# Second products for virtual tiles, and byte distances kept in DRAM, in a three-layer graph network kernel

## The chip, the cores and the metric

The kernel runs on one core of one Trainium2 chip. The metric is the device time of one launch, in microseconds, taken as the median of several runs. One further execution was taken with the hardware profiler; its rows are what is read here. The core's engines, with the names that the profile gives them, are TensorE (PE for matmuls, PEld for its weight loads), VectorE (DVE), ScalarE (ACT), GpSimd (POOL) and SyncE (SP), which here only issues DMAs.

## The reference

A graph has 6250 nodes with 128 features each and 200,000 edges, sorted by their destination. After a layer norm and a ReLU, three layers follow. Each takes for every node the maximum, feature by feature, over the rows of its edges' sources (0 where a node has no edge), and puts that and the node's own row through two linear maps. Widths are 128, 256, 256 and 128.

```python
def _sage_conv(x, src, dst, Wl, bl, Wr):
    agg = jax.ops.segment_max(x[src], dst, num_segments=x.shape[0])
    agg = jnp.where(jnp.isfinite(agg), agg, 0.0)
    return agg @ Wl + bl + x @ Wr
...
h = jnp.maximum(_layernorm(x, axis=-1), 0.0)
h = jax.nn.leaky_relu(_sage_conv(h, src, dst, Wl1, bl1, Wr1), NEG_SLOPE)
h = jax.nn.leaky_relu(_sage_conv(h, src, dst, Wl2, bl2, Wr2), NEG_SLOPE)
h = jax.nn.leaky_relu(_sage_conv(h, src, dst, Wl3, bl3, Wr3), NEG_SLOPE)
return x + h
```

Degrees are uneven: destinations are drawn as the square of a uniform number, so the first nodes have far more edges than the last.

## The kernel before

**Tiles.** The nodes lie in 50 tiles of 127 rows (a table row per node, 128 rows per tile). Sources are taken in 25 pairs of tiles, g = 24 down to 0; the two tiles of a pair are its sides s = 0 and 1. Destinations are *units* of 128 columns: 28 narrow ones (tiles 22 to 49), 19 wide ones (tiles 3 to 21), and 8 *virtual* ones. The first three tiles have too many edges for a row, so `virtual` (L621) cuts their edges into rows of 64, 8 x 128 of them, whose maxima are later joined again by a scan along the rows (`Joined`, L1072).

**Two ways to a maximum.** Most edges are taken by *products*. For each unit and pair the kernel keeps one source per destination column (narrow units), or one per side (wide and virtual units, called *alone*). `one_hot` (L897) makes from the stored index bytes a one-hot matrix of up to 1024 columns on ACT, in two passes: Square of (index minus partition) to bf16, then ReLU of 1 minus it. `products` (L908) multiplies it with the pair's rows on PE, split into a high and a low part, so that the product picks rows exactly; `maxima` (L929) takes the running maximum out of PSUM on DVE. An alone step has one maximum for each side, a narrow step one for both.

Edges whose pair (or side) already has a pick are *leaves*. `flag_rows` (L500) marks them, `pick_rows` (L531) collects them by rounds of eight, `rank_rows` (L549) orders the rows by how many they have, and `send_row` (L603) writes them to lists. A list is walked by *gathers* (`Listed.gather`, L961): one indirect DMA on POOL fetches a table row for each of 128 destinations, and a small memset (L974) follows it. `CAPS` (L55) says how many gathers each list row takes: 147, 181, 230 and 47 for lists 0 to 3 by its sums, 605 a layer. `Listed.maximum` (L976) takes maxima over tiles of gathered rows (8 rows deep in layer 0, 4 in layers 1 and 2; L985, and a tree, L990) and stores the result (L994).

**Groups and steps.** Units are worked in four groups: 24 narrow units (group 0), the 8 virtual (group 1), the 19 wide (group 2) and the last 4 narrow (group 3). List k belongs to group k. A step is one chunk of a group for one pair: 8 units in layer 0, 4 in layers 1 and 2. Layer 0 has 75, 25, 75 and 25 steps in its groups, layers 1 and 2 have 150, 50, 125 and 25.

**Order.** The whole order is written out by the program before it runs. An agenda (L1118 to L1269) puts list work, node work and set-up chores on steps; every engine then runs its own instructions in that order. Gathers of lists 0 to 2 are spread evenly over the steps from the start of a layer to shortly before the end of group 2, with an alone step weighted 1.25 in layers 1 and 2; list 3's lie on group 3. `Node` (L997) is the work of one destination tile: an indirect fetch, a transpose, a merge with the products' maxima, the linear maps, the activation, and the stores of its rows for the next layer. Group 0's nodes start when group 0 ends, one every step in layer 0 and one every second step in layers 1 and 2, so they lie on group 1; group 1's joined tiles lie on group 2, and group 2's nodes on group 3. In layer 0 the flags, selections and index lookups of groups 1 to 3 are chores, spread over steps 0 to 82; `expand` and `lookups` (L697, L717) write index bytes to `idx` in DRAM, one row of bytes per pair.

**Queues.** SP issues nearly all plain DMAs in program order: index loads (`load_idx`, L867, a row of bytes broadcast to all partitions, three blocks ahead), pair loads (`load_pair`, L881, two pairs ahead), list results, node loads and stores. One-hots are made up to six steps ahead of their products (`make_hots`, L1294), at most six at a time.

Of the kernel before, what the change touches and what calls it, by code (L numbers as in the profile page):

```python
# [34 lines left out]
BF16 = mybir.dt.bfloat16  # L35
# [7 lines left out]
P = 128  # L43
# [17 lines left out]
DEEP = (24, 40, 48, 24)  # L61
# [7 lines left out]
def kernel(ctx: ExitStack, tc: tile.TileContext, x, src, dst,  # L69
# [28 lines left out]
    )  # L98
    PLACE, HEAD = {}, []
# [42 lines left out]
    IW = [(len(units) + sum(w == "w" for w, _ in units)) * P for units in GROUPS]  # L142
# [226 lines left out]
    rows_w = edge.tile([P, NW + NV, 2 * CUT], I16, name="rows_w")  # L369
    pos_i = edge.tile([P, NV], I32, name="pos_i")  # L370
# [90 lines left out]
    def rows_of(us):  # L461
        w, i = us[0]
        assert [u for u in us] == [(w, i + j) for j in range(len(us))]
        return (rows_n if w == "n" else rows_w)[:, i : i + len(us), :]
# [252 lines left out]
    def lookups(us, least, s, pool, tags=("v", "v8")):  # L717
# [7 lines left out]
        v8 = pool.tile([NG, n * P], U8, tag=tags[1], name="v8", bufs=1 + (tags[0] == "v"))  # L725
        i = 0
        while i < n:
            k = next(k for k, units in enumerate(GROUPS) if us[i] in units)
            m = 1
            while i + m < n and m < 8 and us[i + m] in GROUPS[k]:  # L730
                m += 1
# [5 lines left out]
            at = GROUPS[k].index(us[i]) + (len(GROUPS[k]) if s else 0)  # L737
# [117 lines left out]
    def chunks(layer, k):  # L855

        n = 8 if widths[layer] == P else 4
        units = GROUPS[k]
        for w in "wn":
            us = [i for i, u in enumerate(units) if u[0] == w]  # L860
            for i0 in range(0, len(us), n):
                part = us[i0 : i0 + n]
                yield (HEAD[k] + part[0]) * P, len(part) * P, part[0], units[part[0]][1] if w == "w" else None
# [23 lines left out]
    def parts_of(k):  # L887

        units = GROUPS[k]
        for w in "wn":  # L890
            us = [i for i, u in enumerate(units) if u[0] == w]
            for i0 in range(0, len(us), HOT // P):
                yield us[i0], len(us[i0 : i0 + HOT // P]) * P, len(units) if w == "w" else 0

    hots, live, done_with = {}, [0], [0, 0]

    def one_hot(layer, k, g, c, w, odd, s):  # L897
# [4 lines left out]
        nc.scalar.activation(sq[:, :w], t[:, at : at + w], AF.Square, bias=near[:, s : s + 1], scale=1.0)  # L902
        hot = work.tile([P, HOT], F32R, tag="hot", name="hot", bufs=HOTS)
        nc.scalar.activation(hot[:, :w], sq[:, :w], AF.Relu, bias=1.0, scale=-1.0)  # L904
# [24 lines left out]
    def maxima(step, s, p, acc):  # L929
        layer, k, g, (_, w, c, odd_u) = step  # L930
# [4 lines left out]
        if g == NG - 1 and (odd_u is None or s == 0):  # L935
# [230 lines left out]
    late_lookups(LISTS[1], 1)  # L1166
    n_soon = len(chores)
# [118 lines left out]
    assert max(IW) >= max(g * w for g, w in zip(GB, IW))  # L1286
# [362 lines left out]
```

## Time and profile before

| | us |
|---|---|
| median of 3 runs | 3579.78 |
| lowest and highest | 3576.79, 3585.17 |
| the profiled execution's own time | 3583.85 |
| its span in the profile | 3582.1 |
| stretch up to the first product | 287.8 |
| layer 0 (to the first product of layer 1) | 1083.7 |
| layer 1 | 1110.9 |
| layer 2 and the end | 1099.7 |

A row of a stage gives busy time for each engine; the share that counts is busy time over the length of that stage, since the engines' limits change from group to group. For POOL each gather also costs a short gap before and after it that is not counted as busy. Mean durations mix shapes where a row says "+2 forms".

### The profile page before, as it was taken

What the parts mean: (1) busy time and instruction counts of PE and PEld (TensorE: products, weight loads), DVE (VectorE), ACT (ScalarE), POOL (GpSimd) and SP (SyncE); (2) the same over time, 40 slices, a digit from 0 to 9 for tenths busy, and PEclk for the clock granted to TensorE, in tenths of its full rate; (3) what the DMA queues carried; (4) which work ended last, traced back from release to release, by engine and by line L of the source; (5) the groups of instructions that cost most, each with busy time, mean ns of one, the idle gap of its engine ahead of it and who ended that gap; (6) DMA issues with size and microseconds to landing.
All of it is one profiled execution on the core that took longest, in us unless ns stands there. A gap on an engine that the chain in (4) does not pass through costs nothing.

```text
span 3582.1 us, 37453 instructions
## 1 busy us (share of the span) xinstructions
PE 2378.9 (66%) x8912; PEld 1680.0 (47%) x8912; DVE 2594.4 (72%) x4077; ACT 2460.1 (69%) x3433; POOL 2837.5 (79%) x4030
## 2 busy tenths in 40 slices
PE   1025632557567567888778687769888777677767
PEld 1013421334334335666555455547666555455545
DVE  6557899987556535666667899955666678799964
ACT  5108952769779758998655587757998856477754
POOL 5578894888888873888876788883888888878884
PEclk9986865769767779999889899989999989899989
DMA  9114320338644366555577665578555567565566
GB/s 288 43 20 111 100 76 14 93 98 265 155 129 125 109 188 184 157 171 159 183 227 233 174 186 175 167 212 281 163 162 165 157 212 239 159 168 171 172 188 195
DMA packets 295272, 579.84 MB, mean 162 GB/s; under 512 B 58529, under 2 KB 155669, under 8 KB 294403
## 3 DMA queue, kind: packets, MB, share of 16 engines
q1 hardware_dynamic: 203331, 347.72, 29.7%
q0 software_dynamic: 91648, 229.44, 24.6%
q8 instruction: 75, 1.23, 0.1%
q14 instruction: 154, 1.26, 0.1%
q10 hardware_dynamic: 64, 0.20, 0.0%
HBM read 486.57 MB, written 90.55 MB: 161 GB/s over the span
## 4 chain that ended last, share of the span: by engine, by line
POOL 27%; DVE 22%; PE 14%; issue 14%; ACT 10%; DMA 10%; another core or an unknown queue 1%; SPq 1%; POOLq 0%; DVEq 0%; ACTq 0%
POOL g L970 18%; DVE acc L938 8%; PE pg L921 8%; POOL pace_t L974 7%; ACT sq L902 6%; DMA g<-table,let 5%; ACT hot L904 3%; PE z_p L1043 2%; DVE g L985 2%; DVE g L990 1%; PE z_p L1045 1%; DVE acc L541 1%; DVE acc L539 1%; DMA agg<-best,end_i 1%
## 5 line engine op out<-in xcount | busy, mean ns | idle before, releaser
L921 PE MATMUL pg<-hot,pair_sb 128*128 128x512 f32 x7000 | 2045.9, 440 | 540.3 <-DVE acc L938 243.4
L970 POOL DMA_INDIRECT g<-table,let x1815 | 1830.8, 1009 | 451.0 <-issue 285.2
L921 PEld LDWEIGHTS pg<-hot,pair_sb 128*128 128x128 f32 x7000 | 1397.5, 212 | 1050.5 <-ACT hot L904 293.7
L938 DVE TENSOR_TENSOR acc<-acc,pg 128x1024 f32<-128x1024 f32 (+3 forms) x1314 | 1488.5, 1161 | 309.0 <-PE pg L921 205.9
L904 ACT ACTIVATE hot<-sq 128x1024 fp32r<-128x1024 bf16 (+2 forms) x1200 | 1126.5, 939 | 367.8 <-PE pg L921 298.4
L902 ACT ACTIVATE sq<-idx_sb,near 128x1024 bf16<-128x1024 uint8 (+2 forms) x1200 | 1218.7, 1016 | 15.5 <-POOL pace_t L974 15.5
L974 POOL MEMSET pace_t<- 128x300 bf16 x1815 | 664.0, 366 | 0.9
L985 DVE TENSOR_TENSOR g<-g 128x1024 f32<-128x1024 f32 (+4 forms) x277 | 290.6, 1049 | 209.9 <-DMA g<-table,let 192.8
L1047 ACT COPY s<-z_p 127x256 f32<-127x256 f32 (+1 forms) x150 | 49.9, 333 | 368.4 <-PE z_p L1045 230.6
L990 DVE TENSOR_TENSOR g<-g 128x256 f32<-128x256 f32 (+3 forms) x355 | 175.7, 495 | 83.1 <-DMA g<-table,let 55.9
L1014 POOL DMA_INDIRECT agg<-best,end_i x141 | 140.5, 997 | 95.2 <-PE aT_p L1030 35.5
L959 ACT ACTIVATE let<-ell 128x4 int32<-128x4 int16 (+3 forms) x516 | 92.8, 189 | 86.9 <-DMA ell<-picks 86.9
L1030 PE MATMUL aT_p<-ident,agg 128*128 128x128 f32 x250 | 57.7, 297 | 141.4 <-DMA agg<-best,end_i 112.2
L1043 PE MATMUL z_p<-wr,hT_in 128*128 128x256 f32 (+1 forms) x500 | 148.6, 418 | 4.6 <-DMA hT_in<-across 4.5
L1036 DVE TENSOR_TENSOR mz<-acc,aT_p 128x256 f32<-128x256 f32 (+1 forms) x141 | 52.4, 371 | 131.3 <-PE aT_p L1030 89.3
L1045 PE MATMUL z_p<-wl,mz 128*128 128x256 f32 (+1 forms) x500 | 121.1, 359 | 8.0 <-DVE mz L1036 3.6
L1030 PEld LDWEIGHTS aT_p<-ident,agg 128*128 128x128 f32 x250 | 34.3, 148 | 170.2 <-DMA agg<-best,end_i 114.6
L605 POOL DMA_INDIRECT picks<-picked,to_i x55 | 59.3, 1078 | 64.7 <-DVE rank_h L581 48.1
L1043 PEld LDWEIGHTS z_p<-wr,hT_in 128*128 128x128 f32 x500 | 86.9, 217 | 34.2 <-issue 12.7
L1045 PEld LDWEIGHTS z_p<-wl,mz 128*128 128x128 f32 x500 | 92.3, 210 | 20.9 <-DVE mz L1036 4.4
L830 PE MATMUL hT_p<-ident,h 128*128 128x128 f32 x200 | 44.9, 309 | 82.8 <-DVE mz L1036 44.3
L348 POOL DMA_INDIRECT win_d<-in_dst_dram,win_i x50 | 52.3, 1046 | 44.0 <-ACT junk_w L353 14.7
(259 smaller groups left out, 1133.5 us busy)
## 6 DMA issues: line engine op xcount, KB each, us to landing
pair_sb<-pair SPq DMA_DIRECT2D x200, 512.0 KB
idx_sb<-idx SPq DMA_DIRECT2D x75, 608.0 KB
g<-table,let POOLq DMA_INDIRECT x1815
idx_sb<-idx SPq DMA_DIRECT2D x75, 384.0 KB
pair_sb<-pair SPq DMA_DIRECT2D x100, 256.0 KB
pair<-pr SPq DMA_DIRECT2D x100, 256.0 KB
idx_sb<-idx SPq DMA_DIRECT2D x75, 256.0 KB
best<-g SPq DMA_DIRECT2D x110, 128.0 KB
```

The costliest lines, as they stand in the source:

```text
L902: nc.scalar.activation(sq[:, :w], t[:, at : at + w], AF.Square, bias=near[:, s : s + 1], scale=1.0)
L904: nc.scalar.activation(hot[:, :w], sq[:, :w], AF.Relu, bias=1.0, scale=-1.0)
L921: nc.tensor.matmul(to, pr[:, s, i, kk * P : (kk + 1) * P], hot[:, o : o + bw], start=((alone or s == 0) and i == 0), stop=((alone or s == ...
L938: nc.vector.tensor_max(to, to, of)
L959: nc.scalar.activation(let[:, :n], ell[self.k][:, q, j : j + n], AF.Identity, scale=1.0)
L970: nc.gpsimd.indirect_dma_start(out=self.tiles[q, b][:, i, :], out_offset=None, in_=tables[self.layer], in_offset=bass.IndirectOffsetOnAxis ...
L974: nc.gpsimd.memset(pace_t, 0.0)
L985: nc.vector.tensor_max(base[:, : i + 1, :], base[:, : i + 1, :], g[:, : i + 1, :])
L990: nc.vector.tensor_max(base[:, :h, :], base[:, :h, :], base[:, w - h : w, :])
L1014: nc.gpsimd.indirect_dma_start(out=self.agg[:, : self.F], out_offset=None, in_=of, in_offset=bass.IndirectOffsetOnAxis(ap=at, axis=0),)
L1043: nc.tensor.matmul(z_p, self.hT[:, i, :], wr[layer][:, i, :], start=False, stop=False)
L1045: nc.tensor.matmul(z_p, self.m[:, i, :], wl[layer][:, i, :], start=False, stop=(i == K - 1))
```

## The change

Virtual units get a *second product*. Where two or more edges of a virtual row have their source in the same pair and side beyond the first picks, one more of them per pair is taken out of the leaves and put into a row of its own, `rows_x`. `EXTRA` holds 8 further units ("x", v), which share the accumulator columns of the virtual units; `PLANES` is `GROUPS` with these added to group 1. An x unit is worked like a narrow one (one pick for both sides, one maximum a step). So list 1 gets shorter: its `CAPS` row sums to 86 in place of 181, and its depth `DEEP` is 24 in place of 40. Group 1 has 50 steps in layer 0 and 100 in layers 1 and 2. Its one-hots go from two to four for each pair, and the x units' lookup is one more chore, before step 40.

The second part changes how one-hots are made. In layer 0 the first pass is Abs to bytes (`away`, three buffers) in place of Square to bf16; the second pass reads these bytes. Each tile of bytes is also stored to DRAM (`far`) by SP, at the time when the next one-hot is issued. In layers 1 and 2 `load_idx` loads these distances, for both sides, in place of the broadcast index bytes, and a one-hot is the second pass alone.

```diff
-    (37, 30, 29, 27, 26, 23, 8, 1),
+    (22, 15, 14, 12, 11, 9, 2, 1),
...
-DEEP = (24, 40, 48, 24)
+DEEP = (24, 24, 48, 24)
...
+    EXTRA = [("x", v) for v in range(NV)]
+    PLANES = [units + (EXTRA if k == 1 else []) for k, units in enumerate(GROUPS)]
...
+    DW = [2 * len(units) * P for units in PLANES]
+    far = [dram.tile([P, NG, DW[k]], U8, name=f"far{k}") for k in range(len(GROUPS))]
...
+        if wide and us[0][1] >= NW:
+            c, seen = S(1, I32, n, J), S(2, I32, n, J)
+            nc.vector.memset(b[:, :, J - 1 :], 0)
+            nc.vector.tensor_copy(c, b)
+            repeated(seen, c, J)
+            nc.vector.tensor_tensor(b, b, c, op=OP.bitwise_xor)
+            x = rows_of([("x", i - NW) for _, i in us])
+            nc.vector.tensor_scalar(f, b, 0.0, float(PAST), op0=OP.is_equal, op1=OP.mult)
+            nc.vector.tensor_tensor(x, f, r[:, :, :J], op=OP.max)
+            nc.vector.tensor_scalar(f, b, 0.0, float(PAST), op0=OP.not_equal, op1=OP.mult)
+            nc.vector.tensor_tensor(r[:, :, :J], f, r[:, :, :J], op=OP.max)
+            b = c
...
-        n, w = len(gs), IW[k]
+        n, w = len(gs), DW[k] if layer else IW[k]
...
+        if layer:
+            nc.sync.dma_start(t[:, : n * w].rearrange("p (g w) -> p g w", w=w), far[k][:, g0 : g0 + n, :])
+        elif n == 1:
...
-        at = of + (c + (odd if s else 0)) * P
-        sq = work.tile([P, HOT], BF16, tag="sq", name="sq", bufs=2)
-        nc.scalar.activation(sq[:, :w], t[:, at : at + w], AF.Square, bias=near[:, s : s + 1], scale=1.0)
+        put = 2 * c * P + s * w
+        if layer == 0:
+            at = of + (c + (odd if s else 0) + (NV if PLANES[k][c] in EXTRA else 0)) * P
+            away = work.tile([P, HOT], U8, tag="away", name="away", bufs=3)[:, :w]
+            nc.scalar.activation(away, t[:, at : at + w], AF.Abs, bias=near[:, s : s + 1], scale=1.0)
+            if unsent:
+                nc.sync.dma_start(*unsent.pop())
+            unsent.append((far[k][:, g, put : put + w], away))
+        else:
+            away = t[:, of + put : of + put + w]
         hot = work.tile([P, HOT], F32R, tag="hot", name="hot", bufs=HOTS)
-        nc.scalar.activation(hot[:, :w], sq[:, :w], AF.Relu, bias=1.0, scale=-1.0)
+        nc.scalar.activation(hot[:, :w], away, AF.Relu, bias=1.0, scale=-1.0)
...
     late_lookups(LISTS[1], 1)
+    late_lookups(EXTRA, 0)
     n_soon = len(chores)
```

More of the change, by code (lines that the diff above doesn't have):

```diff
@@ L141 @@
     cols = dram.tile([P, T], I16, name="cols")
-    IW = [(len(units) + sum(w == "w" for w, _ in units)) * P for units in GROUPS]
+    IW = [(len(units) + sum(w == "w" for w, _ in units)) * P for units in PLANES]
     GB = (1, 1, 1, 5)
     idx = [dram.tile([NG, IW[k]], U8, name=f"idx{k}") for k in range(len(GROUPS))]
+    DW = [2 * len(units) * P for units in PLANES]
+    far = [dram.tile([P, NG, DW[k]], U8, name=f"far{k}") for k in range(len(GROUPS))]
     picks = [dram.tile([len(LISTS[k]) * P, DEEP[k]], I16, name=f"picks{k}") for k in range(NL)]
@@ L369 @@
     rows_w = edge.tile([P, NW + NV, 2 * CUT], I16, name="rows_w")
+    rows_x = edge.tile([P, NV, CUT], I16, name="rows_x")
     pos_i = edge.tile([P, NV], I32, name="pos_i")
@@ L463, in rows_of @@
         assert [u for u in us] == [(w, i + j) for j in range(len(us))]
-        return (rows_n if w == "n" else rows_w)[:, i : i + len(us), :]
+        return {"n": rows_n, "w": rows_w, "x": rows_x}[w][:, i : i + len(us), :]
     def count_of(us):
@@ L724, in lookups @@
             nc.vector.tensor_scalar(v, v, float(P), None, op0=OP.add)
-        v8 = pool.tile([NG, n * P], U8, tag=tags[1], name="v8", bufs=1 + (tags[0] == "v"))
+        v8 = pool.tile([NG, n * P], U8, tag=tags[1], name="v8")
         i = 0
         while i < n:
-            k = next(k for k, units in enumerate(GROUPS) if us[i] in units)
+            k = next(k for k, units in enumerate(PLANES) if us[i] in units)
             m = 1
-            while i + m < n and m < 8 and us[i + m] in GROUPS[k]:
+            while i + m < n and m < 8 and us[i + m] in PLANES[k]:
                 m += 1
@@ L736, in lookups @@
             nc.scalar.copy(part.rearrange("g (c k) -> g c k", k=P), p[:, :m, :])
-            at = GROUPS[k].index(us[i]) + (len(GROUPS[k]) if s else 0)
+            at = NV + PLANES[k].index(us[i]) if us[i] in EXTRA else GROUPS[k].index(us[i]) + (len(GROUPS[k]) if s else 0)
             nc.sync.dma_start(idx[k][:, at * P : (at + m) * P], part)
@@ L857, in chunks @@
         n = 8 if widths[layer] == P else 4
-        units = GROUPS[k]
-        for w in "wn":
+        units = PLANES[k]
+        for w in "wnx":
             us = [i for i, u in enumerate(units) if u[0] == w]
@@ L862, in chunks @@
                 part = us[i0 : i0 + n]
-                yield (HEAD[k] + part[0]) * P, len(part) * P, part[0], units[part[0]][1] if w == "w" else None
+                yield part[0] - (NV if w == "x" else 0), len(part) * P, part[0], units[part[0]][1] if w == "w" else None
     pair_q, idx_q = {}, {}
     def load_idx(layer, k, gs):
-        n, w = len(gs), IW[k]
-        assert stored[k] == w
-        t = work.tile([P, max(IW)], U8, tag="idx", name="idx_sb", bufs=AHEAD + 1)
+        n, w = len(gs), DW[k] if layer else IW[k]
+        assert stored[k] == IW[k]
+        t = work.tile([P, max(DW)], U8, tag="idx", name="idx_sb", bufs=AHEAD + 1)
         g0 = min(gs)
-        if n == 1:
+        if layer:
+            nc.sync.dma_start(t[:, : n * w].rearrange("p (g w) -> p g w", w=w), far[k][:, g0 : g0 + n, :])
+        elif n == 1:
             nc.sync.dma_start(t[:, :w], idx[k][g0 : g0 + 1, :].partition_broadcast(P))
@@ L887, in parts_of @@
     def parts_of(k):
-        units = GROUPS[k]
-        for w in "wn":
+        units = PLANES[k]
+        for w in "wnx":
             us = [i for i, u in enumerate(units) if u[0] == w]
             for i0 in range(0, len(us), HOT // P):
-                yield us[i0], len(us[i0 : i0 + HOT // P]) * P, len(units) if w == "w" else 0
+                yield us[i0], len(us[i0 : i0 + HOT // P]) * P, len(GROUPS[k]) if w == "w" else 0
     hots, live, done_with = {}, [0], [0, 0]
+    unsent = []
     def one_hot(layer, k, g, c, w, odd, s):
         t, of = idx_q[layer, k, g]
-        at = of + (c + (odd if s else 0)) * P
-        sq = work.tile([P, HOT], BF16, tag="sq", name="sq", bufs=2)
-        nc.scalar.activation(sq[:, :w], t[:, at : at + w], AF.Square, bias=near[:, s : s + 1], scale=1.0)
+        put = 2 * c * P + s * w
[8 more added lines that the diff above has]
+            away = t[:, of + put : of + put + w]
         hot = work.tile([P, HOT], F32R, tag="hot", name="hot", bufs=HOTS)
-        nc.scalar.activation(hot[:, :w], sq[:, :w], AF.Relu, bias=1.0, scale=-1.0)
+        nc.scalar.activation(hot[:, :w], away, AF.Relu, bias=1.0, scale=-1.0)
         hots[layer, k, g, c, s] = hot
@@ L929, in maxima @@
     def maxima(step, s, p, acc):
-        layer, k, g, (_, w, c, odd_u) = step
+        layer, k, g, (c, w, _, odd_u) = step
         if widths[layer] // P == 2:
@@ L934, in maxima @@
             of, to = p.rearrange("p h c -> p (h c)")[:, :w], acc[:, 0, c * P : c * P + w]
-        if g == NG - 1 and (odd_u is None or s == 0):
+        if g == NG - 1 and c == step[3][2] and (odd_u is None or s == 0):
             nc.vector.tensor_copy(to, of)
@@ L1285 @@
                 jobs_h.append((at_step[layer, k, g, c], len(blocks) - 1, (layer, k, g, c, w, odd, s)))
-    assert max(IW) >= max(g * w for g, w in zip(GB, IW))
+    assert max(DW) >= max(g * w for g, w in zip(GB, DW)) and max(DW) >= max(g * w for g, w in zip(GB, IW))
     loaded = [0]
@@ L1298, in make_hots @@
             _, b, job = jobs_h.pop(0)
+            if job[0] and unsent:
+                nc.sync.dma_start(*unsent.pop())
             load_until(b + 1 + AHEAD)
```

2 lines of the change are left out of this document (1 added, 1 removed).

## The prediction

> **What bounds the kernel now.** I read the page's busy times first, then the granted clock and busy time of each stage, then groups, then single instructions. A *stage* is one group of one layer. Its bounds come from counting L921's 7000 matmuls off in program order: 600, 200, 500, 100 in layer 0 and 1200, 400, 1000, 200 in layers 1 and 2. On the page no engine stands out:
>
> ```profile
> PE 2378.9 (66%) x8912; PEld 1680.0 (47%) x8912; DVE 2594.4 (72%) x4077; ACT 2460.1 (69%) x3433; POOL 2837.5 (79%) x4030
> ```
>
> By stage it is otherwise. The rows below give: stretch, length, busy us of PE, PEld, DVE, ACT, POOL (instructions), granted clock, DMA share, GB/s. In order: layer 0 group 0 up to step 40, its rest, groups 1, 2, 3; then groups 0, 1, 2, 3 of layer 1 and of layer 2.
>
> ```profile
> 287.80:464.90 177.10, 119.25 (x343) 72.15 (x343) 142.62 (x333) 173.36 (x203) 156.90 (x233) 0.80 0.34 99
> 464.90:756.00 291.10, 109.22 (x324) 71.98 (x325) 273.50 (x720) 155.34 (x176) 215.05 (x313) 0.65 0.22 59
> ...
> 756.00:904.50 148.50, 102.52 (x378) 65.78 (x377) 112.01 (x231) 125.83 (x184) 123.83 (x173) 0.86 0.73 216
> 904.50:1246.10 341.60, 206.05 (x568) 132.12 (x566) 193.49 (x251) 279.83 (x401) 300.44 (x441) 0.72 0.44 124
> 1246.10:1371.50 125.40, 75.08 (x252) 44.10 (x253) 45.77 (x106) 75.88 (x152) 81.65 (x112) 0.74 0.67 198
> 1371.50:1735.20 363.70, 310.53 (x1235) 240.69 (x1233) 240.09 (x249) 331.56 (x390) 298.16 (x435) 0.94 0.54 160
> 1735.20:1972.10 236.90, 182.40 (x701) 130.55 (x702) 168.85 (x199) 127.57 (x192) 177.75 (x251) 0.86 0.75 227
> 1972.10:2357.40 385.30, 291.94 (x1084) 199.22 (x1083) 358.65 (x362) 274.62 (x396) 330.43 (x477) 0.93 0.59 174
> 2357.40:2482.40 125.00, 102.35 (x444) 76.95 (x445) 63.78 (x97) 75.41 (x152) 79.92 (x107) 0.90 0.89 277
> 2482.40:2851.90 369.50, 312.02 (x1258) 241.70 (x1256) 241.75 (x251) 335.23 (x395) 297.94 (x435) 0.95 0.54 160
> 2851.90:3049.20 197.30, 143.53 (x656) 104.27 (x657) 163.81 (x199) 110.49 (x146) 172.35 (x238) 0.91 0.71 228
> 3049.20:3444.20 395.00, 295.91 (x1076) 202.27 (x1074) 358.37 (x361) 269.48 (x384) 341.36 (x490) 0.90 0.56 165
> ```
>
> The gathers' pace comes from the timeline of layer 2's group 0, with an ACT one-hot pair beside it:
>
> ```profile
> 2604.03 0.95 POOL L970 DMA_INDIRECT g<-table,let  x1 [0.16 <-issue]
> ...
> 2605.51 0.95 POOL L970 DMA_INDIRECT g<-table,let  x1 [0.16 <-issue]
> ...
> 2604.12 1.13 ACT L902 ACTIVATE sq<-idx_sb,near 128x1024 bf16<-128x1024 uint8 x1
> 2605.28 1.06 ACT L904 ACTIVATE hot<-sq 128x1024 fp32r<-128x1024 bf16 x1
> 2606.25 1.13 ACT L902 ACTIVATE sq<-idx_sb,near 128x1024 bf16<-128x1024 uint8 x1
> ...
> 2609.95 0.95 POOL L970 DMA_INDIRECT g<-table,let  x1 [0.17 <-issue]
> ...
> 2612.26 1.23 DVE L985 TENSOR_TENSOR g<-g 128x1024 f32<-128x1024 f32 x1 [3.51 <-DMA g<-table,let]
> ```
>
> A gather takes 1.48 us (2604.03 to 2605.51); a one-hot of 1024 columns takes 2.13 us of ACT in two passes (2604.12 to 2606.25). The plan puts 558 gathers on the steps of groups 0 to 2. Gathers per stage:
>
> ```profile
> 756.00:904.50 148.50, 69.81 (x71) 0.86 0.73 216
> 904.50:1246.10 341.60, 210.89 (x214) 0.72 0.44 124
> ...
> 1371.50:1735.20 363.70, 219.52 (x218) 0.94 0.54 160
> 1735.20:1972.10 236.90, 112.58 (x114) 0.86 0.75 227
> 1972.10:2357.40 385.30, 235.22 (x233) 0.93 0.59 174
> ```
>
> So group 0 of layers 1 and 2 is paced by POOL (218 x 1.48 = 323 of 364 us) with ACT close behind (332). Group 2 is paced by DVE (359 of 385) and POOL (233 x 1.48 = 345 and 11 joined fetches). Group 1 is full on no engine. In layer 0, group 0 is ACT-bound up to step 40 (173 of 177) and DVE-bound after it (273 of 291, the chores); group 2 is POOL's (214 x 1.48 = 317 of 342) with ACT at 280.
>
> **The change, part by part.** *Gathers.* List 1 falls from 181 to 86, lists 0 to 2 from 558 to 463 a layer. Group 1 gets twice the steps, so the same plan spreads fewer gathers over more steps: weighted steps go from about 354 to 404 in layers 1 and 2 (143 in group 0, 62.5 to 112.5 in group 1, 149 in group 2), 1.58 to 1.15 gathers a step. In layer 0 it is 3.1 to 2.2.
>
> *Group 0, layers 1 and 2.* POOL: 143 x 1.15 x 1.48 = 243 us. ACT: one pass, 150 x 1.06 and the lets, under 190. DVE loses some 13 list maxima, about 225. PE is next: 1200 matmuls, whose dense pitch and busy time are
>
> ```profile
> 2603.60 9.33 PE L921 MATMUL pg<-hot,pair_sb 128*128 128x512 f32 x40 [0.59 <-ACT sq L902]
> ...
> 1371.50:1735.20 363.70, 305.44 (x1201) 0.94 0.54 160
> ```
>
> 0.233 us each in the burst (9.33 / 40), 0.254 by busy time (305 / 1201, which counts pipeline tails of short bursts). 1200 x 0.233 = 280, with 16 for the four nodes of the layer before (an estimate from the rows of a node below) 296, over 0.975 for waits 304. That is -61 in layer 1 and -64 in layer 2, each between -76 (no waits) and -44 (0.254). I take the burst, since the waits for gathers and one-hots that break bursts now are what goes. [...]
>
> *Group 2, layers 1 and 2.* Its maxima stay; gathers go to 149 x 1.15 = 171, POOL to 265, so DVE alone paces it. About 17 list maxima of 1.22 us leave: -20 each (0 to -35).
>
> *Group 1, layers 1 and 2.* Added: per layer 400 matmuls, 50 one-hots of one pass and 50 maxima of 128x1024; 25 pair steps are now 50. The nodes of group 0 hang here, one to two steps, and turn in a ring:
>
> ```profile
> 1907.93 2.35 DVE L938 TENSOR_TENSOR acc<-acc,pg 128x1024 f32<-128x1024 f32 x2 [2.85 <-PE z_p L1045]
> 1910.20 1.22 DVE L985 TENSOR_TENSOR g<-g 128x1024 f32<-128x1024 f32 x1
> 1911.34 0.42 DVE L1054 SCALAR_TENSOR_TENSOR h<-s 127x256 f32<-127x256 f32 x1
> ...
> 1912.14 0.44 PE L830 MATMUL hT_p<-ident,h 128*128 128x128 f32 x2 [2.19 <-DVE mz L1036]
> ...
> 1914.00 2.08 PE L1043 MATMUL z_p<-wr,hT_in 128*128 128x256 f32 x4
> 1915.87 1.36 PE L1045 MATMUL z_p<-wl,mz 128*128 128x256 f32 x4
> ...
> 1918.20 2.35 DVE L938 TENSOR_TENSOR acc<-acc,pg 128x1024 f32<-128x1024 f32 x2 [2.86 <-PE z_p L1045]
> ```
>
> DVE waits for PE, PE for DVE, 10.3 us a turn here, 9.5 on average (236.9 / 25). A turn of two second-product steps has one maximum fewer in the ring: 8.3. 24 nodes take 12 turns of each: 214. The other 52 steps, 13 pairs of tiles, have no node: six maxima at 1.16 (4.65 us for four on this timeline, 2.35 for two above) and five gathers' share of list maxima, 8.5 us of DVE, 8.9 with waits, 116 in all. 330 for 237: +93. In layer 2 a turn is 7.9 (197.3 / 25) and 6.7: 175 + 116 = 291 for 197, +94. Bounds: below, PE's busy time and 93 more (275, 236: +38, +39); above, the free steps at group 2's and group 0's present pace (385 / 125 and 364 / 150), +121. I take the ring, nearest to what the rows show.
>
> *Group 1, layer 0.* One-hots stay at two passes (Abs to bytes for Square) and double: 50 more of 2.13 us, 107 of ACT onto 126 busy of 148. Some 26 steps with nodes stay at 5.9 (154), 24 steps without at 4.6 (two one-hots, lets): 264, +116 (+85 by ACT alone, +149 at the present pace throughout). *Group 2, layer 0:* POOL falls to about 220, so ACT's 280 paces it, 304 with its joined nodes, -38 (-20 to -60). *Group 0, layer 0:* ACT up to step 40 is as it was. The x lookup adds some 21 us of DVE:
>
> ```profile
> L703 DVE TENSOR_SCALAR acc<-rows_w 128x384 int16<-128x384 int16 (+2 forms) x200 | 63.3, 380 | 0.2
> L709 DVE TENSOR_TENSOR acc<-acc 128x960 int16<-128x960 int16 (+4 forms) x130 | 61.8, 475 | 4.5
> ...
> L710 DVE TENSOR_REDUCE least<-acc 128x30 int16<-128x240 int16 (+3 forms) x45 | 19.5, 433 | 1.6
> ```
>
> (145 us for 54 wide units' sides and a few narrow ones, 2.6 each, eight more). It lies before step 40, where DVE is idle 34 of 177 us. The extra flags and the two selection rounds saved per row of list 1 I set against each other. After step 40 fewer list maxima: -5 (-20 to +20). Group 3 everywhere hangs on nodes: 0, and -2 where ACT has one pass.
>
> *Stores and the added wait.* Layer 0 stores 450 tiles of bytes (52 MB) from SP. SP waits for each Abs, and behind it stand index, pair and node loads and best stores; an Abs waits for the store three before. At 2.13 us a one-hot that leaves 3 x 2.13 - 1.13 = 5.3 us. Nearest row: the gather issued at 2609.95, as large (128 rows of 1 KB), had landed by 2612.26, 2.3 us. Hidden, then. Loads of distances: 768 KB for 384 in group 0, but nine gathers of 128 KB a pair become seven: 2.2 MB in 12 us is 180 GB/s, below the 277 seen in group 3.
>
> **Sum.** Layer 0: -5 + 116 - 38 = +73; layer 1: -61 + 93 - 20 - 2 = +10; layer 2: -64 + 94 - 20 - 2 = +8. +91 on the profiled execution's 3583.85 us (span 3582.1) is 3675. That execution is 4 us above the median shown, so 3671.
>
> **Rivals.** *Faster: the added steps fill the ring's waits.* PE waits 2.2 us and DVE 2.9 in each turn; if matmuls and maxima of the new steps slip in there, group 1 costs only its fullest engine: +38, +39 and +85 in place of +93, +94 and +116, in all -50: 3530. It decides once a new step adds less than 1.9 us of PE. Against it: engines run in program order, and nodes are bound to steps, not to time; the free steps come after. 0.14. *PE is not next in group 0.* Then POOL's 243 paces it, 254 with waits, 50 less in each layer: 3571. Against it: no burst is denser than 0.23 us. 0.04. [...] *Stores hold ACT in layer 0.* With SP held elsewhere, as it is now,
>
> ```profile
> SPq L994 <- DVE g L990: 912.1, 122, 35.5
> ```
>
> landings of 6.5 us make a one-hot 2.54 us, 0.4 more on some 330: +132, 3803. From 5.3 us it decides; 2.3 speaks against. 0.10. *One pass buys little:* the doubled bytes or DVE's waits for gathers keep group 0 half way: +62, 3733. 0.08.
>
> **How the numbers follow.** Forecast 0.62 (3620 to 3725, the bounds of group 1 and group 0 not all on one side), the rest unnamed. Range 3565 to 3745: it takes in the second rival and the fourth, leaves out most of the first and the third. A measurement of this kernel tells 0.2% (7 us) from nothing. Faster: 0.14, half of the second, a little of the forecast's lower end: 0.18. Same: 0.06. Slower: 0.76.
>
> **What would show it.** Layer 1 group 0 near 304 us with PE above 0.9 busy; group 1 near 330 with free steps at 2.2 us and DVE full; layer 0 group 1 near 264 with ACT full; layer 0 group 2 ACT-bound. POOL, with 285 gathers fewer, should be near 0.67 busy over the span. Wrong if group 1 of layer 1 is under 290, or POOL still paces group 0, or Abs waits for DMA.

## The result and the profile after

The changed kernel took 3522.2 us (median of four runs, 3516.2 to 3531.8) against 3579.6 for the kernel before (four runs, 3576.8 to 3585.2): a ratio of 0.984, interval 0.9814 to 0.9867. It is faster by 1.6%, where 2.5% slower was forecast. The profiled execution took 3516.2 us (span 3514.4), 68 less than that of before. Of these 68, 22 lie in the stretch up to the first product (287.8 before, 265.8 after), and are not the change's doing: four kernels run on one chip, with second products and without, all have 266 to 270 there.

First the page's busy times (engine, busy us, share of the span, instructions), then the windows of the changed kernel cut at the same places as in the prediction: groups 0 to 3 of layer 0, of layer 1 and of layer 2, the columns as there.

```profile
PE 2570.8 (73%) x9920; PEld 1816.2 (52%) x9920; DVE 2686.4 (76%) x4152; ACT 1894.1 (54%) x2762; POOL 2444.0 (70%) x3460
```

```profile
265.80:771.10 505.30, 250.72 (x674) 149.34 (x675) 415.72 (x1053) 330.22 (x361) 297.06 (x436) 0.68 0.37 102
771.10:1032.80 261.70, 181.13 (x603) 111.31 (x601) 151.20 (x274) 234.44 (x304) 175.69 (x252) 0.86 0.73 205
1032.90:1323.10 290.20, 194.45 (x540) 118.40 (x540) 181.97 (x232) 270.44 (x363) 224.62 (x330) 0.78 0.60 176
1323.10:1439.20 116.10, 79.44 (x253) 44.66 (x253) 45.63 (x105) 81.23 (x163) 61.49 (x81) 0.77 0.83 243
1439.20:1724.10 284.90, 282.69 (x1234) 231.63 (x1233) 224.88 (x231) 162.65 (x220) 226.93 (x331) 0.99 0.69 213
1724.10:2019.30 295.20, 264.66 (x1113) 194.39 (x1112) 236.38 (x264) 127.42 (x208) 208.66 (x292) 0.98 0.76 219
2019.30:2383.50 364.20, 290.52 (x1073) 196.05 (x1071) 340.65 (x339) 139.66 (x222) 261.07 (x376) 0.93 0.52 163
2383.50:2489.80 106.30, 99.17 (x445) 74.86 (x446) 63.48 (x97) 44.78 (x105) 61.86 (x81) 0.97 0.98 328
2489.80:2774.50 284.70, 283.79 (x1258) 232.79 (x1257) 226.67 (x233) 163.70 (x223) 228.52 (x336) 1.00 0.70 218
2774.50:3020.90 246.40, 231.45 (x1065) 173.17 (x1064) 229.35 (x264) 108.42 (x160) 205.77 (x287) 1.00 0.76 222
3020.90:3382.70 361.80, 284.22 (x1066) 190.90 (x1065) 340.01 (x339) 137.47 (x216) 259.38 (x378) 0.94 0.52 161
3382.70:3514.40 131.70, 93.34 (x457) 70.70 (x457) 66.33 (x116) 30.72 (x73) 62.22 (x79) 0.86 0.68 202
```

Read the length against the fullest engine, row by row. Group 0 of layers 1 and 2 is now PE's alone: 282.7 busy of 284.9. Group 2 is DVE's (341 of 364). Group 1 has no full engine, but PE stands at 265 of 295 in layer 1, at a clock of 0.98 where it was 0.86 before, and at 231 of 246 in layer 2. The two tables side by side:

| stage | before | after | measured | forecast |
|---|---|---|---|---|
| start and layer 0, group 0 | 756.0 | 771.1 | +15 | -5 |
| layer 0, group 1 | 148.5 | 261.7 | +113 | +116 |
| layer 0, group 2 | 341.6 | 290.2 | -51 | -38 |
| layer 0, group 3 | 125.4 | 116.1 | -9 | 0 |
| layer 1, group 0 | 363.7 | 284.9 | -79 | -61 |
| layer 1, group 1 | 236.9 | 295.2 | +58 | +93 |
| layer 1, group 2 | 385.3 | 364.2 | -21 | -20 |
| layer 1, group 3 | 125.0 | 106.3 | -19 | -2 |
| layer 2, group 0 | 369.5 | 284.7 | -85 | -64 |
| layer 2, group 1 | 197.3 | 246.4 | +49 | +94 |
| layer 2, group 2 | 395.0 | 361.8 | -33 | -20 |
| layer 2, group 3 | 137.9 | 131.7 | -6 | -2 |
| sum | | | -68 | +91 |

In the first row group 0 itself rose by 37 (468.2 to 505.3); the shorter start hides 22 of it. The forecast is 159 us too high. Half of that, 80, is group 1 of layers 1 and 2; 39 is their group 0, 21 their group 3, 14 their group 2, and 5 is layer 0 with the start before it.

Group 1 splits into the part with nodes and the free steps behind it. These are the two windows of layer 1:

```profile
1724.10:1912.20 188.10, 165.33 (x710) 121.77 (x709) 134.87 (x171) 73.22 (x138) 119.91 (x165) 0.96 0.74 219
1912.20:2019.30 107.10, 99.33 (x405) 72.62 (x404) 101.50 (x93) 54.20 (x70) 88.74 (x128) 1.00 0.79 219
```

The 50 free steps take 2.14 us each (forecast 2.2) with DVE nearly full, 101.5 of 107.1. The nodes' part (the other 50 steps) takes 188 where 214 was forecast for 48. So the free steps were sized rightly, and the ring was not.

Before, a turn of the ring lasted 10.26 us in the rows of the prediction (from the matmul of `wr` at 1914.00 to the next at 1924.26). These windows of the kernel before cut the same stretch every 3.41 us (length, PE's busy time, clock, DMA share, GB/s):

```profile
1902.88:1906.29 3.41, 3.41 (x9) 0.50 0.90 276
1906.29:1909.70 3.41, 3.41 (x17) 1.00 0.87 262
1909.70:1913.11 3.41, 1.22 (x7) 1.00 0.23 82
1913.12:1916.53 3.41, 3.41 (x9) 0.50 0.83 278
1916.53:1919.94 3.41, 3.41 (x17) 1.00 0.86 255
1919.94:1923.35 3.41, 1.23 (x7) 1.00 0.36 121
```

The clock goes 0.50, 1.00, 1.00 and again: one window in three at half, in step with the turn (three windows are 10.24 us). The slow window stands behind the one in which PE, after waiting 2.19 us for DVE, was busy for only 1.22 us of 3.41. In these turns the node's matmuls fall into the slow one: four of them took 2.08 us there, at 0.50. PE's longest wait in a turn was 2.19 us. With the profile cut on the same grid (its records of the clock begin at 230 us, after the change at 211), the clock is 0.50 or 1.00 in 982 windows of 983 (in all 968 after the change). What tells slow windows from fast ones in these traces is how long PE was busy in the window before: a full-speed window in which PE was busy for less than 40% was followed by a half-speed one in 86 cases of 86, one with more than 60% in none of 488; between the two both occur (51 half, 63 full). After the change it is 44 of 44 and none of 581.

In the changed kernel the timeline of PE has this, in a stretch of the same kind:

```profile
1843.93 1.13 PE L1070 MATMUL z_p<-wr,hT_in 128*128 128x256 f32 x4
...
1849.97 0.44 PE L847 MATMUL hT_p<-ident,h 128*128 128x128 f32 x2 [1.05 <-DVE mz L1063]
...
1851.47 1.13 PE L1070 MATMUL z_p<-wr,hT_in 128*128 128x256 f32 x4
...
1856.37 0.44 PE L847 MATMUL hT_p<-ident,h 128*128 128x128 f32 x2
...
1857.88 1.13 PE L1070 MATMUL z_p<-wr,hT_in 128*128 128x256 f32 x4
```

The same four matmuls take 1.13 us, at a clock of 1.00. A turn of two alone steps is 7.54 us (1843.93 to 1851.47), one of two second-product steps 6.41 (to 1857.88). PE's wait for DVE is 1.05 us in the first and gone in the second; it was 2.19. A single wait of 1.05 us leaves PE busy for some 69% of a window (an estimate from 1.05 of 3.41). What left DVE's side is the list maximum ahead of `h` (1910.20 in the prediction's rows, 1.14 us until `h` starts at 1911.34). In this turn after the change there is none:

```profile
1846.89 2.35 DVE L965 TENSOR_TENSOR acc<-acc,pg 128x1024 f32<-128x1024 f32 x2 [1.51 <-PE pg L948]
1849.16 0.42 DVE L1081 SCALAR_TENSOR_TENSOR h<-s 127x256 f32<-127x256 f32 x1
1849.50 0.41 DVE L1063 TENSOR_TENSOR mz<-acc,aT_p 128x256 f32<-128x256 f32 x1
```

So of the 2.72 us between the turns (10.26 to 7.54), 1.14 are the list maximum and the other 1.58 go with the clock.

### The profile page after: what moved, and what is told of

It is laid out like the page before. It is cut to its first block, busy times and chain, and to the rows that moved or that the text cites. A ratio compares the mean times of both kernels' runs of the same rounds, so it can differ in the third digit from the quotient of the medians.

```text
span 3514.4 us, 39180 instructions
## 1 busy us (share of the span) xinstructions
PE 2570.8 (73%) x9920; PEld 1816.2 (52%) x9920; DVE 2686.4 (76%) x4152; ACT 1894.1 (54%) x2762; POOL 2444.0 (70%) x3460
## 5 line engine op out<-in xcount | busy, mean ns | idle before, releaser
L948 PE MATMUL pg<-hot,pair_sb 128*128 128x512 f32 (+1 forms) x8000 | 2257.3, 429 | 536.5 <-ACT hot L931 249.6
L948 PEld LDWEIGHTS pg<-hot,pair_sb 128*128 128x128 f32 x8000 | 1540.3, 204 | 1124.2 <-ACT hot L931 442.3
L997 POOL DMA_INDIRECT g<-table,let x1530 | 1543.9, 1009 | 765.6 <-ACT let L986 320.7
L965 DVE TENSOR_TENSOR acc<-acc,pg 128x1024 f32<-128x1024 f32 (+3 forms) x1439 | 1647.2, 1168 | 484.1 <-PE pg L948 338.3
L931 ACT ACTIVATE hot<-idx_sb 128x1024 fp32r<-128x1024 uint8 (+2 forms) x900 | 827.0, 948 | 732.8 <-PE pg L948 463.1
L924 ACT ACTIVATE away<-idx_sb,near 128x1024 uint8<-128x1024 uint8 (+2 forms) x450 | 464.4, 1032 | 210.1 <-DMA far<-away 178.0
L1001 POOL MEMSET pace_t<- 128x300 bf16 x1530 | 560.3, 366 | 1.0
L931 ACT ACTIVATE hot<-away 128x1024 fp32r<-128x1024 uint8 (+2 forms) x450 | 427.7, 951 | 14.3
L1012 DVE TENSOR_TENSOR g<-g 128x1024 f32<-128x1024 f32 (+6 forms) x218 | 219.6, 1007 | 1.6 <-DMA g<-table,let 1.5
L1017 DVE TENSOR_TENSOR g<-g 128x512 f32<-128x512 f32 (+3 forms) x351 | 172.9, 493 | 10.2
```

Source lines behind the costliest of these rows:

```text
L924: nc.scalar.activation(away, t[:, at : at + w], AF.Abs, bias=near[:, s : s + 1], scale=1.0)
L931: nc.scalar.activation(hot[:, :w], away, AF.Relu, bias=1.0, scale=-1.0)
L948: nc.tensor.matmul(to, pr[:, s, i, kk * P : (kk + 1) * P], hot[:, o : o + bw], start=((alone or s == 0) and i == 0), stop=((alone or s == ...
L965: nc.vector.tensor_max(to, to, of)
L997: nc.gpsimd.indirect_dma_start(out=self.tiles[q, b][:, i, :], out_offset=None, in_=tables[self.layer], in_offset=bass.IndirectOffsetOnAxis ...
L1001: nc.gpsimd.memset(pace_t, 0.0)
```

## The experiments

Each run is compared with the kernel before on the same chip; whole times of different chips are not set against each other, since the kernel before had medians from 3532.9 to 3596.0 us in the four sets of runs. Stage lengths are, with two cautions. The same layer 0 took 1083.7 us in the kernel before and 1102.7 in a kernel below (the one with matmuls that nobody reads) that differs from it in layer 1 alone, so some 20 us between chips say nothing there. And group 1 of layer 1 took 288.8 to 302.8 us in six kernels whose layers 1 and 2 are the same. "Layer 0" below is without the start, which differs by chip (235 to 237 us in one set, 264 to 270 in two others): 1083.7 for before, 1173.4 after.

**The two parts apart.** The second products alone, with two-pass one-hots everywhere:

```diff
...
+        sq = work.tile([P, HOT], BF16, tag="sq", name="sq", bufs=2)
+        nc.scalar.activation(sq[:, :w], t[:, at : at + w], AF.Square, bias=near[:, s : s + 1], scale=1.0)
...
-        nc.scalar.activation(hot[:, :w], away, AF.Relu, bias=1.0, scale=-1.0)
+        nc.scalar.activation(hot[:, :w], sq[:, :w], AF.Relu, bias=1.0, scale=-1.0)
```

> The second products alone: one-hots in two passes in all layers, index bytes loaded as before, no distances stored. Theory A (each part lifts one of two limits that lie close together: POOL and ACT in group 0 of layers 1 and 2): group 0 of layer 1 stays near 345 us, since ACT's two passes (150 x 2.13 us and the lets) now pace it alone; group 1 of layer 1 near 300; 3590 to 3630 us in all, slower than before. Rival B (the gathers were the limit and the second pass was hidden): group 0 near 290 us, total 3490 to 3530.

And the distances alone:

```diff
-    (22, 15, 14, 12, 11, 9, 2, 1),
+    (37, 30, 29, 27, 26, 23, 8, 1),
...
-DEEP = (24, 24, 48, 24)
+DEEP = (24, 40, 48, 24)
...
-    EXTRA = [("x", v) for v in range(NV)]
+    EXTRA = []
...
```

> The stored distances alone: no second products, lists of 558 gathers in groups 0 to 2 as before, one pass in layers 1 and 2. Theory A: POOL alone paces group 0 of layers 1 and 2 (218 gathers of 1.48 us, 323 us): 330 to 345 us each against 364 and 369; group 2 hardly moves; layer 0 up to 15 us longer by its stores; 3530 to 3560 us in all. Rival B' (ACT was the limit): group 0 near 290 us, total 3440 to 3480.

Second products alone: 3572.5 us, ratio 0.9927 (0.99 to 0.9954), a little faster where slower was expected. Distances alone: 3636.0, ratio 1.0104 (1.0081 to 1.0126), slower where faster was expected. The ratios multiply to 1.003; together the parts give 0.984. Group 0 of layer 1 shows why. This is its window with second products alone, and group 1's behind it:

```profile
1376.10:1706.80 330.70, 302.81 (x1235) 225.34 (x1234) 226.78 (x231) 322.59 (x364) 225.30 (x330) 0.99 0.52 156
1706.80:2005.20 298.40, 267.03 (x1113) 196.19 (x1112) 236.35 (x264) 239.51 (x313) 199.31 (x287) 0.97 0.72 206
```

And with distances alone, group 0:

```profile
1422.60:1786.60 364.00, 305.90 (x1235) 237.61 (x1233) 239.49 (x249) 164.92 (x237) 299.46 (x435) 0.95 0.60 184
```

ACT halved (165) and 364.0 us, as before: POOL still paces the stage. It stands until 1449.1, 26 us into the stage, in a wait of 36.9 us for ACT (a list's indices), and from there runs 337 us with some 2 us of waits for other engines; the 330 to 345 expected left that standing time out. POOL relieved (225): 330.7, and now ACT paces it, at 323. Both: 284.9, and PE paces it. Two limits close to each other have to go together, and the gain of each alone says little. Group 1 of layer 1 is 298.4 without any change to its one-hots, so its 295 does not come from the one pass. In layer 0 the second products alone give 1105.8 (group 0 472.9, then 251.0, 278.4, 103.5), the distances alone 1155.3, and there the distances only cost.

**The list's length by itself.** The changed kernel with list 1 as long as before, 95 gathers a layer more; the added ones fetch the floor row, and two small constant tiles lie in another pool for room:

```diff
-    (22, 15, 14, 12, 11, 9, 2, 1),
+    (37, 30, 29, 27, 26, 23, 8, 1),
...
-DEEP = (24, 24, 48, 24)
+DEEP = (24, 40, 48, 24)
...
```

> The whole change, but with the list lengths of before (181 gathers for list 1, the ones too many fetch the floor row): second products without fewer gathers. Theory C (the nodes' turn in group 1 got short because PE's clock stays up): group 1 of layer 1 stays at 290 to 305 us and its clock above 0.95; group 0 near 300 us by POOL (about 195 gathers); total 3570 to 3600 us. Rival D (the turn got short because fewer list maxima stand in it): group 1 of layer 1 at 320 us or more.

One run: 3767.4 us, span 3765.6, far above the 3570 to 3600 expected; group 0 of layer 1 takes 329.0 where 300 was expected. Stage by stage it is 251 us above the changed kernel (65 in layer 0, 89 and 97 in layers 1 and 2): 0.88 us for each of 285 gathers. So it is the shorter list that pays for the second products. Whether gathers of many rows would cost as much as these, which all fetch one, was not measured. Group 1 of layer 1:

```profile
1833.80:2153.60 319.80, 276.37 (x1114) 202.43 (x1113) 244.20 (x269) 127.68 (x215) 237.31 (x338) 0.93 0.84 210
```

319.8 against 295.2 (288.8 to 302.8 in the six), at 0.93 against 0.98: with the gathers the list maxima are back, and with them half-clock time. (Half-clock time, an estimate, is 2 x (1 - clock) x length, with the clock taken as 0.50 or 1.00 as in the windows above: 66 us in this group before, 12 after, 45 here.) A theory that the clock alone was cured by denser matmuls expected over 0.95 here; it fails.

**Clock or list maximum?** Into the kernel before, eight matmuls whose product nobody reads, ahead of each transpose of group 0's nodes in layer 1:

```diff
+            if self.layer == 1 and self.k == 0:
+                f_p = psum.tile([P, 512], F32, tag="z", name="f_p")
+                for _ in range(8):
+                    nc.tensor.matmul(f_p, ident_b, mask_v[:, :512], start=True, stop=True)
```

> The kernel before, with eight bf16 matmuls of 128x512 without use ahead of the transposes of each of group 0's nodes in layer 1, at the place where PE waits 2.2 us for DVE. Theory C: PE's clock no longer drops to half in every turn; group 1 of layer 1 falls from 237 to 195-215 us though PE has more to do, its granted clock goes from 0.86 to above 0.95, and the total is 3545 to 3565 us. Rival D: the turn is DVE's and PE's work, 237 us or more, total 3580 or more.

The group's window and PE's timeline in it:

```profile
1732.40:1960.00 227.60, 199.95 (x875) 136.64 (x885) 168.78 (x199) 129.64 (x192) 179.64 (x251) 0.95 0.78 239
```

```profile
1885.00 0.44 PE L830 MATMUL hT_p<-ident,h 128*128 128x128 f32 x2 [0.43 <-DVE mz L1036]
1886.51 1.13 PE L1043 MATMUL z_p<-wr,hT_in 128*128 128x256 f32 x4
...
1893.67 0.44 PE L830 MATMUL hT_p<-ident,h 128*128 128x128 f32 x2 [0.43 <-DVE mz L1036]
1895.19 1.13 PE L1043 MATMUL z_p<-wr,hT_in 128*128 128x256 f32 x4
```

The clock rises from 0.86 to 0.95 and the four matmuls go from 2.08 to 1.13 us; a turn with a list maximum falls from 10.26 to 8.68, the 1.58 read off above. But turns that had been 7.54 become 8.02 by the added matmuls, one turn takes 14.27 for a reason not found, and the group ends at 227.6 (236.9 before), between the two expectations. The whole took 3577.2 us in one run, against 3596.0 and an expected 3545 to 3565. The clock is a part, not all.

Then the other half: the kernel before with only the order within a step changed, so that a node's work stands ahead of the list maxima (and of layer 0's set-up chores and the starts of joined tiles, which share their place).

```diff
-        act(MAXIMA, ROWS, REST, LINEAR, MERGE, SOONER, GATHER, FETCH)
+        act(ROWS, REST, LINEAR, MERGE, SOONER, MAXIMA, GATHER, FETCH)
```

> The kernel before with one edit of order: within a step the nodes' work on DVE, ACT and PE stands ahead of the list maxima. Theory D (the 1.2 us list maximum that stands ahead of the node's two DVE operations is part of each turn of the ring): the turn in layer 1 group 1 loses 1.1 us at half clock and more where the clock then stays up, 237 us falls to 200-220, layer 2's group 1 little, layer 0's group 1 a little; total 20 to 45 us below the kernel before. Theory C alone: 230 us or more.

DVE's timeline in its ring, and the group's window:

```profile
1851.29 2.35 DVE L938 TENSOR_TENSOR acc<-acc,pg 128x1024 f32<-128x1024 f32 x2 [0.79 <-PE pg L921]
1853.56 0.42 DVE L1054 SCALAR_TENSOR_TENSOR h<-s 127x256 f32<-127x256 f32 x1
1853.89 0.41 DVE L1036 TENSOR_TENSOR mz<-acc,aT_p 128x256 f32<-128x256 f32 x1
1854.23 1.22 DVE L985 TENSOR_TENSOR g<-g 128x1024 f32<-128x1024 f32 x1
```

```profile
1691.80:1894.70 202.90, 161.91 (x702) 118.38 (x702) 167.50 (x199) 125.07 (x190) 177.09 (x247) 0.95 0.85 266
```

The list maximum is done behind `mz`, while PE works: 202.9 us for 236.9, turns of 7.54, clock 0.95, with every gather and every maximum still there. Moving 1.1 us out of the ring also brought the clock back (0.86 to 0.95). Layer 2's group 1 stayed at 197.1 (197.3): there the ring was not what held it, and POOL was, as shown further down. One run: 3499.6 us against 3532.9.

**What the stores cost layer 0.** Between the second products alone and the whole change lie 68 us of layer 0 (1105.8 to 1173.4), on two chips. On one chip, the distances alone stand 53 above the layer 0 of before (1155.3 and 1102.7). ACT's wait for a free byte buffer stands in the changed kernel's waits (us in all, times, longest):

```profile
ACT away L924 <- DMA far<-away: 178.0, 49, 27.1
```

SP issues a store behind whatever else is in its order, where its waits for list maxima alone came to 213.7 us in layer 0, up to 32.1 us each. So in two kernels the store was issued by ACT behind the second pass, or two more buffers were given:

```diff
-            if unsent:
-                nc.sync.dma_start(*unsent.pop())
-            unsent.append((far[k][:, g, put : put + w], away))
...
+        if layer == 0:
+            nc.scalar.dma_start(far[k][:, g, put : put + w], away)
```

> The changed kernel with layer 0's stores of distances issued by ACT itself, right behind the second pass, in place of SP. Theory E (the stores cost layer 0 some 60 us because they stand in SP's order behind best stores that wait for DVE, so ACT waits for its byte buffers): ACT's waits for these stores in layer 0's group 0, 140 us now, all but go; start and group 0 of layer 0 end near 745 us in place of 771; layer 0 some 40 to 60 us shorter; total 3455 to 3480 us. Rival F (the stores cost DMA time, not order): layer 0 stays within 10 us, total 3510 to 3530 us.

```diff
...
-            away = work.tile([P, HOT], U8, tag="away", name="away", bufs=3)[:, :w]
+            away = work.tile([P, HOT], U8, tag="away", name="away", bufs=5)[:, :w]
```

> The changed kernel with five byte buffers in place of three (two small constants moved to make room). Theory E: two one-hots more, some 4 us, do not cover waits of up to 27 us: 10 to 25 us less, 3495 to 3510 us. Rival G (landings are just late, 5 to 8 us): most of the 60 us of layer 0 goes, 3460 to 3480 us.

Issued by ACT, the same row reads

```profile
ACT away L924 <- DMA far<-away: 8.6, 11, 1.8
```

and layer 0 takes 1148.4, 25 less (40 to 60 expected); ratio 0.9739 (0.9715 to 0.9763). With five buffers the wait is still 135.7 us, and layer 0 takes 1143.3, 30 less (10 to 25 expected); ratio 0.9743 (0.9721 to 0.9765). So 169 us of wait taken away and 42 taken away gave about the same 25 to 30 us: most of that wait was no loss. Some 40 us were still to be explained. Two kernels asked whether they are the stores or the Abs to bytes: the second products alone with Abs in place of Square and no store, and the kernel with ACT's stores made to store every tile twice, the second time to a tensor that nobody reads.

```diff
-        sq = work.tile([P, HOT], BF16, tag="sq", name="sq", bufs=2)
-        nc.scalar.activation(sq[:, :w], t[:, at : at + w], AF.Square, bias=near[:, s : s + 1], scale=1.0)
+        sq = work.tile([P, HOT], U8, tag="away", name="away", bufs=3)
+        nc.scalar.activation(sq[:, :w], t[:, at : at + w], AF.Abs, bias=near[:, s : s + 1], scale=1.0)
```

> Second products alone as in e1_second_only, but the first pass writes bytes by Abs in place of bf16 by Square, and nothing is stored. Theory F': layer 0 ends near 1376 us as there (1366 to 1386). Theory H: 1405 or more.

```diff
+    far_2 = [dram.tile([P, NG, DW[k]], U8, name=f"far_2{k}") for k in range(len(GROUPS))]
...
             nc.scalar.dma_start(far[k][:, g, put : put + w], away)
+            nc.scalar.dma_start(far_2[k][:, g, put : put + w], away)
```

> Stores from ACT as in e5_act_store, and each tile of distances stored a second time to a tensor that nobody reads. Theory F' (what still separates layer 0 there from the second products alone, 1416 against 1376 us at its end, is the stores' own DMA and issue time): another 25 to 50 us, layer 0 ends at 1440 to 1465. Theory H (it is something else, the bytes in place of bf16 or the order): within 10 us of 1416.

One run of each, on the same chip. Without stores layer 0 takes 1085.8 (1105.8 with Square, on another chip), so the Abs costs nothing that shows. With stores doubled it takes 1224.3: 138 above the kernel without, so 69 for a set of stores, and 76 above the 1148.4 of one set on another chip, more than the 25 to 50 expected. Group 2 of layer 0 for both, first without stores, then with two:

```profile
952.00:1227.40 275.40, 192.50 (x540) 115.73 (x540) 182.11 (x232) 268.80 (x364) 223.90 (x330) 0.79 0.43 128
```

```profile
1015.20:1331.70 316.50, 214.71 (x541) 126.94 (x541) 182.12 (x232) 277.44 (x363) 224.21 (x332) 0.71 0.69 211
```

The work of DVE and POOL is the same, ACT is busy 9 us more, and the stage is 41 us longer with the DMA share at 0.69 for 0.43. It is the stores themselves. Whether it is the DMA engines' time or the issue of a store on an engine's queue was not separated.

**ACT in group 1 of layer 0.** The second-product one-hots of layer 0 taken from ACT, made by one comparison on DVE:

```diff
...
+        if layer == 0 and PLANES[k][c] in EXTRA:
+            nc.vector.tensor_scalar(hot[:, :w], t[:, at : at + w], spot[:, s : s + 1], None, op0=OP.is_equal)
+        else:
+            nc.scalar.activation(hot[:, :w], away, AF.Relu, bias=1.0, scale=-1.0)
...
```

> The changed kernel, but in layer 0 the x units' one-hots are made by DVE in one comparison of index bytes with the partition's place; ACT makes only their distances. If ACT's passes are what group 1 of layer 0 pays for (theory of the prediction): 50 passes of 1.06 us go, 262 us falls to 215-230 us and the total to 3480-3495 us. If nodes and DMA bound it: 255 us or more, total 3515 or more.

```profile
771.80:1017.90 246.10, 171.83 (x604) 112.84 (x602) 187.44 (x325) 185.00 (x254) 186.65 (x247) 0.85 0.76 217
```

246.1 for 261.7, with ACT at 185 for 234: 49 us of ACT gone and 16 of time, between the 215 to 230 of "ACT paces it" and the 255 of "it does not". No engine is full in that row; the nodes' ring holds it here too (argued, not tested). The whole: 3498.2 us, ratio 0.979 (0.9768 to 0.9813). With ACT's stores added:

> Both edits: stores from ACT and x one-hots of layer 0 on DVE. Theory E and the prediction's theory together: layer 0 80 to 95 us shorter, 3425 to 3450 us in all. With rivals F and the nodes' bound: 3510 to 3530 us.

3473.3 us, ratio 0.9706 (0.968 to 0.9732), layer 0 at 1142.7: 31 shorter than in the changed kernel, where 80 to 95 were expected of the two theories together. Against ACT's stores alone, on the same chip, DVE's one-hots take only 8 us off group 1 of layer 0 (261.0 to 253.0).

**Together.** That kernel with the reordering of the ring as well (node work ahead of list maxima, the diff shown above):

> The edits of e7 and the order of e10 on the changed kernel: stores from ACT, x one-hots of layer 0 on DVE, node work ahead of list maxima. Some 10 to 25 us under e7's ratio of 0.971: 0.963 to 0.969. If the order matters only at half clock, no change against e7.

3415.6 us (3409.0 to 3419.1), ratio 0.9671 (0.9648 to 0.9693), as expected: faster than both kernels. That the order adds to the last kernel is not clear from these ratios, whose intervals overlap; group 1 of layer 1 shows it. Groups 0 and 1 of its layer 1:

```profile
1361.40:1643.60 282.20, 281.65 (x1234) 230.67 (x1233) 224.87 (x231) 162.48 (x220) 226.48 (x335) 0.99 0.69 216
1643.60:1923.20 279.60, 258.09 (x1114) 190.39 (x1114) 236.28 (x264) 127.35 (x208) 204.44 (x288) 1.00 0.77 230
```

Group 1 falls to 279.6 (295.2 after, 288.8 to 302.8 in the six) at a full clock. PE is at 258 of it, so little is left but to give PE less.

## Why the prediction was wrong

**Group 1, layers 1 and 2: the step that failed (80 of 159 us).** It set the turns of the new steps at the present mean, 9.5 us in layer 1, less one maximum (8.3), and called this "the ring, nearest to what the rows show". The mean was not the ring's own. In layer 1 (35 of the 80) it held list maxima on the way of `h` and `mz`, and half-clock windows which the waits behind them brought on. The ring by itself is 7.54 and 6.41 us; the difference of the two kinds, one maximum, was right. The change took list maxima away along with the gathers, and the nodes' part ended at 188 for 214. These are the groups of list maxima on DVE in layer 1's group 1 before, and in its nodes' part after:

```profile
L985 DVE TENSOR_TENSOR g<-g 128x1024 f32<-128x1024 f32 (+3 forms) x22 | 25.2, 1147 | 3.3 <-DMA g<-table,let 3.3
```

```profile
L1012 DVE TENSOR_TENSOR g<-g 128x1024 f32<-128x1024 f32 (+2 forms) x14 | 15.5, 1104 | 0.0
```

22 became 14, over the same 24 nodes. The run with the list maxima moved out of the ring and nothing else (202.9 for 236.9) shows this step's mechanism; the run with the old lists (319.8) shows it from the other side. The cue was in the quoted row: the four matmuls of `wr` at 2.08 us are nearly twice the 1.13 that they take at full clock, and the granted clock of 0.86 stood in the window.

In layer 2 (45 of the 80) the mean of 7.9 was not the ring's but POOL's, and "Group 1 is full on no engine" was the misreading. These are POOL's groups in that stage before:

```profile
L970 POOL DMA_INDIRECT g<-table,let x107 | 111.0, 1037 | 21.1 <-issue 19.8 <-DVE acc L938 0.6 <-ACT hot L904 0.3
L974 POOL MEMSET pace_t<- 128x300 bf16 x107 | 39.1, 365 | 0.1
L1014 POOL DMA_INDIRECT agg<-best,end_i x24 | 23.1, 964 | 4.0 <-issue 3.6 <-DVE acc L938 0.2 <-DVE g L990 0.2
```

Its 173 us of work and 25 of idle time, nearly all of it the short gaps between its own instructions (0.16 us ahead of a gather, none between it and the memset behind it), fill the 197.3; its waits for other engines come to under 2 us. The reordered kernel, with as many gathers, stayed at 197.1. The change took gathers away (67 stand in the nodes' part for 107), and POOL's limit with them. The nodes' part came to 138 us where 175 was forecast, with PE nearly full:

```profile
2774.50:2912.80 138.30, 131.24 (x656) 99.95 (x655) 125.08 (x167) 55.15 (x92) 114.68 (x157) 1.00 0.75 228
```

**Group 0, layers 1 and 2: right mechanism, size off (39 us).** "PE is next" holds to the letter, with 282.7 of 284.9 busy. The mis-sized term is 1200 x 0.233 over 0.975 plus nodes, 304 us. In layer 1 the matmuls of products took 277 (280 in the sum), the nodes' 6 more (16), and 2 were left for waits (8). The bound of -76 does not follow from these terms either: 296 without waits is -68 and -74. PE's timeline after:

```profile
1499.71 12.63 PE L948 MATMUL pg<-hot,pair_sb 128*128 128x512 f32 x55
```

0.230 us a matmul (12.63 / 55) at a clock of 1.00, and no gap to divide by. So the rival that PE is not next does not hold: 0.23 is the pace of these matmuls in a burst without a gap, and the stage's granted clock was 0.99.

**Groups 2 and 3.** Group 2 is DVE's as forecast: -21 and -33 for -20 each. Group 3 of layer 1 fell 19 us where 2 were given to the one pass. That size came with the second products: 105.4 with them alone, 106.7 with the old lists, 122.7 with the distances alone. The granted clock went with it (0.90 before, 0.97 after), and so did the list-3 gathers that fell into the stage (42 before, 29 after). Why is open.

**Layer 0: right as a sum, by luck.** With the start before it, it measured +68 where +73 was forecast, of which the shorter start gave -22. The layer itself rose by 90. On one chip the second products alone leave it 3 us above that of before (1105.8 and 1102.7): group 0 -11, group 1 +90, group 2 -54, group 3 -22, where -5, +116, -38 and 0 were forecast. The stores, set at nothing ("Hidden, then"), cost the rest, by the three pairs above 53 to 69 us. The rival that stores hold ACT was real (178 us of waits, up to 27.1 us each; "Abs waits for DMA" was one of the prediction's signs of being wrong) and its price of 132 some twice too high; its mechanism, the wait, is the smaller part of it (25 us).

**The rival that was nearest in time,** the added steps filling the ring's waits (3530), is not what happened: the free steps stand behind the nodes at 2.14 us each, and layer 0's group 1 rose by 113, not 85. Its prices for group 1 of layers 1 and 2, +38 and +39 by PE's busy time, were nearer to the measured +58 and +49 than the forecast's +93 and +94, but for another reason: the waits went away, they were not filled. That one pass buys little is true only where POOL still paces, as in the kernel with distances alone.

## What to carry to other kernels

Before the pace of a dependent loop between two engines is carried over to new work, take it apart: subtract what merely stands in its order, and read the granted clock in windows as short as a turn. Add an engine's short gaps to its busy time before calling it free: POOL at 172 of 197 us was full. A piece of work that nobody waits for goes behind the work that the other engine waits for; moving 1.1 us of it was worth 34 us in a stage of 237 here. And where two engines pace a stage within a tenth of each other, cost the edits together: alone they gave -0.7% and +1.0%, together -1.6%.

## What the hardware showed that was not expected

With both profiles cut every 3.41 us, the clock went with PE's busy share of the window before: behind a window at full speed with PE busy for under 40%, half speed came every time (86 of 86 before, 44 of 44 after), behind one with over 60% never (0 of 488 and 0 of 581). In the ring of layer 1 before, one wait of 2.2 us a turn left PE busy for 1.22 us of one window in three, the next ran at half speed (0.50), and a turn took 10.26 us. With waits of 1.05 us a turn the clock stayed near full (0.95 in the reordered kernel's group 1).

Storing 450 tiles of bytes (350 of them 128 KB, 52 MB in all) beside running loads lengthened layer 0 by some 53 to 69 us, though a gather of 128 KB had landed in 2.3 us.

The kernel before had medians from 3532.9 to 3596.0 us in four sets of runs, 1.8% apart; within a set its times were within 0.4% of the median. Experiments in one set therefore tell more than whole times from two.
